# Twelve-layer decoder on one core: the additive mask of two cross-attentions moves from TensorE into VectorE's maximum

## The chip, the cores and the metric

The kernel runs on one core of a Trainium2 chip. The metric is the device time of one execution in microseconds (us). Engines are named as in the profile: PE is TensorE's matmul, PEld its weight load, DVE is VectorE, ACT is ScalarE, POOL is GpSimd, SP is SyncE, which issues the transfers here.

## What is computed

A decoder of four blocks, each with a self-mixing layer, a cross-attention to a context of 154 rows and a feed-forward layer; each of the twelve is followed by a residual and a layer norm. There are 4 batch elements, 512 rows, width 128, and 16 heads of width 8. The change touches the four cross-attentions. The masked ones (L1 and L3) are, cut to what matters:

```python
def _L1_xattn_ref(q, k, v, mask, Wq, bq, Wk, bk, Wv, bv, Wo, bo):
    qh, kh, vh = (proj(q, Wq, bq), proj(k, Wk, bk), proj(v, Wv, bv))
    scores = jnp.einsum('bhqd,bhkd->bhqk', qh, kh) / jnp.sqrt(jnp.float32(D_K))
    scores = jnp.where(mask[:, None] == 0, jnp.float32(-1000000000.0), scores)
    attn = jax.nn.softmax(scores, axis=-1)
    ctx = jnp.einsum('bhqk,bhkd->bhqd', attn, vh)
    concat = ctx.transpose(0, 2, 1, 3).reshape(bs, -1, INPUT_DIM)
    return concat @ Wo.T + bo

x = _layernorm(x + _L1_xattn_ref(x, ctx_1024, ctx_1024, mask_BxSxS2_ik1, ...), axis=-1)
```

L3 is the same without biases and with a mask of the other sense. L2 has biases and no mask. L0 has neither mask nor output projection, and an inner layer norm with gamma and beta: `x = z + decoded`, normed, times gamma plus beta, before the outer residual and norm.

## The kernel before

**Layers and pieces.** Every layer is a generator that yields small pieces. The driver runs the pieces of one layer in its main phase, and between two layers it mixes the tail of the old one with the start of the new one by a hand-written pattern of letters. Engines take their instructions in the order in which the pieces record them; nothing is reordered later, so each engine has a fixed queue.

**A cross-attention (`cross_attention`, L816)** works on 16 units per layer: a batch element times a group of four heads. Two things are computed for the scores of a unit. First (`half`, with a = n + 2) the scores with rows on the partitions, `scx`, from which only the row maxima are taken. Later (with n) the transposed scores `stx`, from which ScalarE takes the exponentials `pTx`. Between them the negated maxima `top` are split into three bf16 parts on GpSimd (`split_maxima`, L488 to L491), turned over on TensorE (`link_maxima`, L499) and added on VectorE into spare rows of the query operand (L501), so that the matmul of the transposed scores subtracts the maximum by itself.

**A step n** (`step`) records in this order: half 0 (scores of unit n + 2, transposed scores of unit n), `sums` (L991, products with the values for unit n − 1), `link_maxima` for n + 1, agenda pieces (division of an older unit's output, output projection and norm once per batch element, preparation of the next one), half 1, `more_sums` (L1000), `left` (L977, L979, the last 26 keys), `split_maxima` for n + 2. Steps run from −2; units 0 and 1 get their maxima in steps −2 and −1.

**One half of a masked layer before the change.** For each of two pairs of row tiles (qp) a PSUM tile `scx` of 128 x (2 x 2 x 154) f32 is taken. `psum2` hands these out in turn from two buffers, so a half's tiles are those of the half before it. TensorE first writes the mask into each (L936, identity times the bf16 mask `mq`, 308 columns, 2 matmuls per tile), then the mask into `stx` (L945), then adds the scores (L950: 8 matmuls of 154 columns, 4 per tile) and the transposed scores (L958). VectorE then takes one maximum over each tile:

```python
for qp, sc in enumerate(scs):
    nc.vector.tensor_reduce(
        ops.maxima(a)[:, 2 * qp : 2 * qp + 2, 2 * gp : 2 * gp + 2].rearrange("p i r -> p r i"),
        sc, AX.X, ALU.max, negate=True,
    )
```

**Other places.** L0's output path (`more_sums`, shuffled form): VectorE transposes (L1012) and takes reciprocals (L1014), GpSimd divides (L1015); once per batch element GpSimd adds the residual (L1026), VectorE takes the statistics, and GpSimd applies the norm (L1030 through `applied`, L346), gamma, beta and the residual. `send` (L396) projects queries or keys into PSUM, ScalarE adds the bias and scales (L408), with a scaled copy of the bias from VectorE where the scale is not one (L406), and GpSimd splits the result in three (L409 to L412) for transfers that SP issues (L416). The sends for L2's cross-attention are recorded during the layer before it (L2_attn).

Of the kernel before, what the change touches and what calls it, by code (L numbers as in the profile page):

```python
# [12 lines left out]
BF16 = mybir.dt.bfloat16  # L13
# [3 lines left out]
ALU = mybir.AluOpType  # L17
# [4 lines left out]
P = 128  # L22
B, S, D = 4, 512, 128
NT = S // P
H, DK = 16, 8
KC = 154
# [148 lines left out]
def decoder_kernel(ctx: ExitStack, tc: tile.TileContext, x, ctxT, mask1, mask3, packs, offsets, out, layers):  # L175
# [217 lines left out]
    Q_ROWS, K_ROWS = ((1, 1, 3), (6, 1, 2), (0, 1, 1)), ((0, 3, 3), (1, 6, 2), (2, 1, 1))  # L393
    SLOT = 32

    def send(far, order, w, rhs, scale, bias, raw, part, on=nc.gpsimd, by=nc.sync):  # L396

        n = rhs.shape[-1]
        pj = psum_t("ps_proj", kind="a" if "a" in ring else "t")
        nc.tensor.matmul(pj[:, :n], lhsT=w, rhs=rhs, start=True, stop=True)  # L400
        if bias is None:
            nc.scalar.activation(raw, pj[:, :n], AF.Copy, scale=scale)
        else:
            if scale != 1.0:
                scaled_bias = small.tile([P, 1], F32, tag="sb", name="sb", bufs=2)
                nc.vector.tensor_scalar(scaled_bias, bias, scale, None, ALU.mult)  # L406
                bias = scaled_bias
            nc.scalar.activation(raw, pj[:, :n], AF.Identity, bias=bias, scale=scale)  # L408
        on.tensor_copy(part[:, 0, :], raw)  # L409
        on.tensor_tensor(raw, raw, part[:, 0, :], ALU.subtract)  # L410
        on.tensor_copy(part[:, 1, :], raw)
        on.tensor_tensor(part[:, 2, :], raw, part[:, 1, :], ALU.subtract)  # L412
        for i, (at, gap, m) in enumerate(order):
            for r in range(2):
                rows = far[r].rearrange("(s k) p c -> (k p) s c", k=DK)
                by.dma_start(  # L416
                    rows[:, at : at + gap * (m - 1) + 1 : gap, :],
                    part[64 * r : 64 * r + 64, i : i + 1, :].to_broadcast([64, m, n]),
                )
# [7 lines left out]
    def sends(i, x_T):  # L427

        name, w = layers[i], weights[layers[i]]
        if name.endswith("xattn"):  # L430
            scale = 1.0 if name == "L0_xattn" else DK ** -0.5

            def key(b):
                return lambda room: send(
                    far_kc[b], K_ROWS, w["wk"], ctx_sb[:, b, :], 1.0, w.get("bk"), *room(KC)
                )

            def query(b):
                return lambda room: send(
                    far_q[i % 2][b], Q_ROWS, w["wq"], x_T[:, b, :], scale, w.get("bq"), *room(S)  # L440
                )

            return [x for b in range(B) for x in ((-1, ("k", b), key(b)), (b, ("q", b), query(b)))]
        if name == "L3_attn":
            xd = []

            def down(room):
                xd.append(room("xd"))
                pd = psum_t("xd", kind="a" if "a" in ring else "t")
                nc.tensor.matmul(pd, lhsT=w["wd"], rhs=x_T[:, 0, :], start=True, stop=True)  # L450
                evacuate(xd[0], pd)

            scale = DK ** -0.25
            return [
                (0, "down", down),
                (0, ("q", 0), lambda room: send(far_q[i % 2][0], Q_ROWS, w["wq"], xd[0], scale, None, *room(S))),
                (0, ("k", 0), lambda room: send(far_k[0], K_ROWS, w["wk"], xd[0], scale, None, *room(S))),
            ]
        return []
# [356 lines left out]
    def cross_attention(w, cur, new, last, room, scale, mask=None, shuffled=False):  # L816
# [15 lines left out]
        made = {}  # L832
        agenda = Agenda()
        units = 4 * B

        def masks(b):
            bt = slice(b * NT, (b + 1) * NT)
# [88 lines left out]
        def half(a, n, gp):  # L926

            scs, sts = [], []
            if a is not None:
                ma, ja = made[a // 4], a % 4  # L930
                for qp in range(2):
                    sc = psum2("scx")[:, :, : 2 * KC].rearrange("p r (i k) -> p r i k", k=KC)
                    scs.append(sc)
                    if mask is not None:
                        for r in range(2):
                            nc.tensor.matmul(  # L936
                                sc[:, r], lhsT=identb, rhs=ma["mq"][:, 2 * qp : 2 * qp + 2, :], start=True,
                                stop=False, skip_group_check=True,
                            )
            if n is not None:  # L940
                mn, jn = made[n // 4], n % 4
                sts = [psum_a("stx") for r in range(2)]
                if mask is not None:
                    for st in sts:
                        nc.tensor.matmul(st, lhsT=identb, rhs=mn["mT"], start=True, stop=False, skip_group_check=True)  # L945
            for qt in range(NT):
                for r in range(2):
                    if a is not None:
                        rows = slice(64 * r, 64 * r + 64)
                        nc.tensor.matmul(  # L950
                            scs[qt // 2][:, r, qt % 2, :], lhsT=ma["q"][rows, 2 * ja + gp, qt * P : (qt + 1) * P],
                            rhs=ma["k"][rows, 2 * ja + gp, :], start=(mask is None), stop=True,
                            skip_group_check=True,
                        )
                for r in range(2):
                    if n is not None and qt == 0:
                        rows, p = slice(64 * r, 64 * r + 64), 2 * jn + 1 - gp
                        nc.tensor.matmul(  # L958
                            sts[r], lhsT=mn["k"][rows, p, :P], rhs=mn["q"][rows, p, :],
                            start=(mask is None), stop=True, skip_group_check=True,  # L960
                        )
            for qp, sc in enumerate(scs):
                nc.vector.tensor_reduce(  # L963
                    ops.maxima(a)[:, 2 * qp : 2 * qp + 2, 2 * gp : 2 * gp + 2].rearrange("p i r -> p r i"),
                    sc, AX.X, ALU.max, negate=True,
                )
            for r, st in enumerate(sts):
                pT = work[0].tile([P, S], F32, tag="pTx", name="pTx", bufs=8)
                nc.scalar.activation(pT, st, AF.Exp)  # L969
                weights_of[n, 2 * (1 - gp) + r] = pT  # L970
# [25 lines left out]
        def more_sums(n):  # L996
            b, j = divmod(n, 4)
            m = made[b]
            av = m["av"]
            nc.tensor.matmul(  # L1000
                av, lhsT=m["v2"][:, j].rearrange("p g k -> p (g k)"), rhs=weights_of.pop((n, 4)),
                start=False, stop=True, skip_group_check=True,
            )
            if not shuffled:
                avs = copied(av, keep)
                agenda.add(n + 2, [lambda: divided(avs, m["o"], j)])
                if j == 3:
                    agenda.add(n + 3, out_pieces(b, m["o"], w, keep, cur, new, last, split=True))
                return

            ot = keep.tile([P, 16, 32], F32, tag="ot", name="ot", bufs=2)
            nc.vector.transpose(ot.rearrange("p s k -> p (s k)"), av.rearrange("p (q s) -> p s q", s=16))  # L1012
            rec = small.tile([P, 16], F32, tag="recx", name="recx")
            nc.vector.reciprocal(rec, ot[:, :, DK])  # L1014
            nc.gpsimd.tensor_tensor(  # L1015
                m["zt"][:, j, :].rearrange("p (s d) -> p s d", d=DK), ot[:, :, :DK],
                rec[:, :, None].to_broadcast([P, 16, DK]), ALU.mult,
            )
            if j == 3:
                zt = m["zt"]  # L1020
                xs = cur["x"][:, b * NT : (b + 1) * NT, :]
                ys = keep.tile([P, NT, D], F32, tag="ys", name="ys")
                stats = []

                def inner():
                    nc.gpsimd.tensor_tensor(zt, zt, xs, ALU.add)  # L1026
                    stats.extend(ln_stats(zt, NT, "i"))

                def outer():
                    applied(ys, zt, NT, *stats, on=nc.gpsimd)  # L1030
                    nc.gpsimd.tensor_tensor(ys, ys, w["gamma"][:, None, :].to_broadcast([P, NT, D]), ALU.mult)
                    nc.gpsimd.tensor_tensor(ys, ys, w["beta"][:, None, :].to_broadcast([P, NT, D]), ALU.add)
                    nc.gpsimd.tensor_tensor(ys, ys, xs, ALU.add)

                agenda.add(n + 2, [inner, outer] + finish_pieces(b, ys, new, last, split=True))
# [1370 lines left out]
```

## Time and profile before

| what | value |
|---|---|
| median of 3 runs (lowest, highest) | 2720.16 us (2719.19, 2727.39) |
| time of the profiled execution | 2720.02 us |
| its span, first to last instruction | 2718.2 us |
| PE busy, share of the span | 2445.7 us, 90% |
| DVE busy | 1681.6 us, 62% |
| ACT busy | 1251.3 us, 46% |
| POOL busy | 1071.5 us, 39% |
| mean granted TensorE clock | 0.954 |
| first and last row of the mask matmuls L936 | start at 846.5 and 2429.5 us |
| rows of L0's division L1015 | start at 273.1 to 375.3 us |

The page gives busy times as shares of the whole span; the layers have different limits, so what a change in one layer is worth is read from windows cut inside that layer. The two masked cross-attentions lie at about 845 to 985 us (L1) and 2305 to 2450 us (L3); L0's lies at about 245 to 390 us. A group row gives the line, engine, operation, output and inputs with shapes, then count, busy time and mean duration, then idle time of the engine just before and what ended it.

### The profile page before, as it was taken

To read this page: it belongs to the slowest core of one execution; us is meant where nothing else is said; L and a number is where in the kernel's file an instruction comes from. 1 tells how busy PE (TensorE), PEld (TensorE's weight loads), DVE (VectorE), ACT (ScalarE), POOL (GpSimd) and SP (SyncE) were. 2 spreads that over 40 slices of the span, in tenths; PEclk is the share of its full clock that TensorE was granted. 3 is DMA by queue.
4 is the path that set the end of the run, shared out by engine and by line. 5 is a ranking of instruction groups with operands and counts; after the bars stand their busy time and mean duration, and the time that the engine had idled before them with its cause. 6 is when DMAs were issued, how large, how long until landed. Compare 5 with 4: busy or idle time off the path is not lost. (4 is left out here: it accounts for less than half of the span.)

```text
span 2718.2 us, 38015 instructions
## 1 busy us (share of the span) xinstructions
PE 2445.7 (90%) x14378; PEld 1179.3 (43%) x14378; DVE 1681.6 (62%) x2872; ACT 1251.3 (46%) x2533; POOL 1071.5 (39%) x1406
## 2 busy tenths in 40 slices
PE   5898789988877989999999999998988999899998
PEld 1233234433333444444444555554455233445665
DVE  6796741188997665555445555556755887664444
ACT  3775432377652433333233555553543777343221
POOL 2342540157675326555452444443355342320000
PEclk7998989989989999999999999998997899899999
DMA  5421310000002400000000000002102240410000
GB/s 153 116 79 57 100 35 0 1 0 1 0 16 75 146 7 1 1 1 1 1 1 1 15 10 3 12 13 72 49 1 59 71 120 20 132 33 1 5 5 8
DMA packets 75559, 96.40 MB, mean 35 GB/s; under 512 B 23664, under 2 KB 62320, under 8 KB 75376
## 3 DMA queue, kind: packets, MB, share of 16 engines
q1 hardware_dynamic: 74224, 92.14, 11.7%
q8 instruction: 113, 1.85, 0.3%
q10 hardware_dynamic: 1152, 1.84, 0.2%
q14 instruction: 70, 0.57, 0.1%
HBM read 63.92 MB, written 33.49 MB: 36 GB/s over the span
## 5 line engine op out<-in xcount | busy, mean ns | idle before, releaser
L1164 POOL TENSOR_TENSOR pr<-pr,zs 128x1024 f32<-128x1024 f32 x192 | 237.1, 1252 | 234.2 <-DVE zs L1161 185.4
L670 DVE TENSOR_REDUCE top<-sc 128x2 f32<-128x1024 f32 x256 | 300.8, 1215 | 46.1 <-PE sc L666 43.2
L691 ACT ACTIVATE pT<-st 128x512 f32<-128x512 f32 x512 | 276.2, 598 | 88.2 <-PE st L682 85.1
L1155 ACT ACTIVATE pr<-scc,nm 128x256 f32<-128x256 f32 (+3 forms) x384 | 198.2, 526 | 173.2 <-DVE nm L1149 107.7
L1149 DVE TENSOR_REDUCE nm<-scc 128x2 f32<-128x1024 f32 x192 | 153.5, 820 | 167.5 <-PE scc L1137 166.3
L963 DVE TENSOR_REDUCE top<-scx 128x4 f32<-128x616 f32 x256 | 191.4, 791 | 90.1 <-PE scx L950 79.2
L969 ACT ACTIVATE pTx<-stx 128x512 f32<-128x512 f32 x256 | 139.1, 596 | 213.4 <-PE scx L950 128.2
L2137 POOL TENSOR_TENSOR hh<-hh,cs 128x1024 f32<-128x1024 f32 x64 | 149.3, 2354 | 74.5 <-DVE hh L2133 50.2
L1288 DVE TENSOR_TENSOR vtmp<-psve,gm 128x1024 f32<-128x1024 f32 x64 | 78.3, 1224 | 153.7 <-PE psve L1283 58.4
L705 PE MATMUL av<-pT,vbuf 128*32 128x256 f32 x2048 | 162.8, 393 | 8.6 <-ACT avs L505 8.6
L337 POOL TENSOR_TENSOR rsf<-mvf,eps 128x4 f32<-128x4 f32 x48 | 9.8, 204 | 394.3 <-DVE mvf L335 393.3
L488 POOL CAST nmP<-top 128x16 bf16<-128x16 f32 x96 | 25.3, 264 | 344.4 <-DVE top L963 180.3
L1131 PE MATMUL scc<-k,q 64*128 64x512 f32 (+3 forms) x768 | 143.9, 472 | 6.5 <-ACT pr L1155 2.7
L1180 PE MATMUL ptc<-ident,pr 128*128 128x128 f32 x960 | 137.8, 281 | 10.5 <-POOL pr L1164 8.9
L2133 DVE TENSOR_TENSOR_SCAN hh<-da,pb 128x1024 f32<-128x1024 f32 x64 | 142.6, 2269 | 0.0
L1293 POOL TENSOR_TENSOR vtmp<-vtmp 128x512 f32<-128x512 f32 x60 | 76.1, 1269 | 162.3 <-DVE vtmp L1288 137.7
L666 PE MATMUL sc<-kP,qP 64*128 64x512 bf16 x512 | 106.0, 412 | 33.9 <-DVE top L670 16.6
L1283 PE MATMUL psve<-w_L_ffn,xT 128*128 128x512 f32 x256 | 123.1, 605 | 14.5 <-ACT pr L1155 11.2
L2146 PE MATMUL acc<-hh,ident 128*128 128x512 f32 x256 | 132.9, 646 | 3.1 <-DVE yt L2155 1.9
L1193 PE MATMUL avc<-pT,v 128*64 128x512 f32 (+3 forms) x768 | 131.4, 449 | 0.5 <-DVE pT L1516 0.5
L1180 PEld LDWEIGHTS ptc<-ident,pr 128*128 128x128 f32 x960 | 103.1, 141 | 50.5 <-issue 26.4
L1326 PE MATMUL yT<-gT,w_L_ffn 128*128 128x512 f32 x256 | 123.4, 605 | 0.0
(417 smaller groups left out, 5065.1 us busy)
## 6 DMA issues: line engine op xcount, KB each, us to landing
qP<-far_q SPq DMA_DIRECT2D x24, 768.0 KB, 5.8
w_L_ffn<-in_L_ffn SPq DMA_DIRECT2D x24, 512.0 KB, 6.2
far_q<-part SPq DMA_DIRECT2D x44, 192.0 KB, 2.8
qP<-far_q SPq DMA_DIRECT2D x24, 256.0 KB, 4.2
far_q<-part SPq DMA_DIRECT2D x44, 128.0 KB, 2.4
kP<-far_k SPq DMA_DIRECT2D x7, 768.0 KB, 5.1
kP<-far_kc SPq DMA_DIRECT2D x16, 231.0 KB, 4.6
w_L_attn<-in_L_attn SPq DMA_DIRECT2D x6, 512.0 KB, 6.5
```

The costliest lines, as they stand in the source:

```text
L670: return lambda: nc.vector.tensor_reduce(top[:, qt, 2 * gp : 2 * gp + 2], sc, AX.X, ALU.max, negate=True)
L691: nc.scalar.activation(pT, st, AF.Exp)
L705: nc.tensor.matmul(m["av"][32 * g : 32 * g + 32, part], lhsT=m["v"][:, kt, 4 * j + g, :], rhs=weights_of[s, g][:, part], start=(kt == 0 an ...
L963: nc.vector.tensor_reduce(ops.maxima(a)[:, 2 * qp : 2 * qp + 2, 2 * gp : 2 * gp + 2].rearrange("p i r -> p r i"), sc, AX.X, ALU.max, negat ...
L969: nc.scalar.activation(pT, st, AF.Exp)
L1131: nc.tensor.matmul(sc[:, r, at : at + n], lhsT=q[rows, qt * P : n], rhs=k[rows, :n], start=(i == 0), stop=False, skip_group_check=True,)
L1149: nc.vector.tensor_reduce(nm[:, i, :], sc[:, :, at : at + (qt + 1) * P], AX.X, ALU.max, negate=True)
L1155: nc.scalar.activation(pr[:, r, at:to], sc[:, r, at:to], AF.Exp, bias=nm[:, i, r : r + 1], accum_out=zs[:, i, r : r + 1],)
L1164: nc.gpsimd.tensor_tensor(pr[:, :, at : at + n], pr[:, :, at : at + n], zs[:, i, :, None].to_broadcast([P, 2, n]), ALU.mult)
L1180: nc.tensor.transpose(pt[:, r, to : to + P], self.pr[u, p][:, r, lo : lo + P], ident)
L2133: nc.vector.tensor_tensor_scan(flat, das[g % 2][:, c].rearrange("p n t -> p (n t)"), pbs[c].rearrange("p n t -> p (n t)"), 0.0, ALU.mult, ...
L2137: nc.gpsimd.tensor_tensor(m["h", j][c], m["h", j][c], m["C", j], ALU.mult)
```

## The change

In the masked layers the mask is no longer written into `scx` by TensorE. The score matmuls start the accumulation themselves. In place of one `tensor_reduce` over a tile of four blocks of score rows there are four `tensor_tensor_reduce`, each of which adds 154 mask values to 154 scores, multiplies by −1, writes the elements to a tile that nobody reads (`unused`, one buffer) and takes the minimum into one column of `top`. The mask for the transposed scores (L945, L977) stays on TensorE. In L0 the division and the inner norm go from GpSimd to VectorE. In L2 the sends' bias and scale go from ScalarE to VectorE.

```diff
-    def send(far, order, w, rhs, scale, bias, raw, part, on=nc.gpsimd, by=nc.sync):
+    def send(far, order, w, rhs, scale, bias, raw, part, on=nc.gpsimd, by=nc.sync, biased=nc.scalar):
...
+        elif biased == nc.vector:
+            nc.vector.tensor_scalar(raw, pj[:, :n], bias, scale, ALU.add, ALU.mult)
         else:
             if scale != 1.0:
...
+            biased = nc.vector if name == "L2_xattn" else nc.scalar
...
+        unused = pool.tile([P, KC], BF16, name="unused", bufs=1) if mask is not None else None
...
-                    if mask is not None:
-                        for r in range(2):
-                            nc.tensor.matmul(
-                                sc[:, r], lhsT=identb, rhs=ma["mq"][:, 2 * qp : 2 * qp + 2, :], start=True,
-                                stop=False, skip_group_check=True,
-                            )
...
-                            rhs=ma["k"][rows, 2 * ja + gp, :], start=(mask is None), stop=True,
+                            rhs=ma["k"][rows, 2 * ja + gp, :], start=True, stop=True,
...
             for qp, sc in enumerate(scs):
+                if mask is not None:
+
+                    for i in range(2):
+                        for r in range(2):
+                            nc.vector.tensor_tensor_reduce(
+                                unused, sc[:, r, i], ma["mq"][:, 2 * qp + i, :], -1.0, 3.0e38, ALU.add, ALU.min,
+                                ops.maxima(a)[:, 2 * qp + i, 2 * gp + r : 2 * gp + r + 1],
+                            )
+                    continue
...
-            nc.gpsimd.tensor_tensor(
+            nc.vector.tensor_tensor(
                 m["zt"][:, j, :].rearrange("p (s d) -> p s d", d=DK), ot[:, :, :DK],
...
-                    applied(ys, zt, NT, *stats, on=nc.gpsimd)
+                    applied(ys, zt, NT, *stats)
```

In the built program each `tensor_tensor_reduce` is two VectorE instructions: one over 128 x 154, and one that writes a 128 x 1 column of `top`. Each of the first kind waits for a VectorE semaphore, because it writes the same `unused` as the one before.

| engine | instructions that go | instructions that come |
|---|---|---|
| PE | 256 matmuls L936, with their weight loads | none |
| DVE | 128 `tensor_reduce` over 128 x 616, 4 scaled biases | 512 over 128 x 154, 512 of 128 x 1, 16 divisions, 16 norm applications, 8 biases |
| ACT | 8 biases | none |
| POOL | 16 divisions, 16 norm applications | none |

More of the change, by code (lines that the diff above doesn't have):

```diff
@@ L431, in sends @@
             scale = 1.0 if name == "L0_xattn" else DK ** -0.5
+            biased = nc.vector if name == "L2_xattn" else nc.scalar
             def key(b):
                 return lambda room: send(
-                    far_kc[b], K_ROWS, w["wk"], ctx_sb[:, b, :], 1.0, w.get("bk"), *room(KC)
+                    far_kc[b], K_ROWS, w["wk"], ctx_sb[:, b, :], 1.0, w.get("bk"), *room(KC), biased=biased
                 )
@@ L439, in query @@
                 return lambda room: send(
-                    far_q[i % 2][b], Q_ROWS, w["wq"], x_T[:, b, :], scale, w.get("bq"), *room(S)
+                    far_q[i % 2][b], Q_ROWS, w["wq"], x_T[:, b, :], scale, w.get("bq"), *room(S), biased=biased
                 )
```

## The prediction

> **What bounds the kernel now.** I read the page's engine shares, then cut windows inside the two masked layers, and there read the chain of waits. The chain in L3's cross-attention (start us, us, what):
>
> ```profile
> 2349.80 0.63 PE scx L936 x4
> 2350.43 0.43 PE stx L945 x2
> 2350.86 0.17 PE scx L950 x2
> 2351.03 0.21 PE stx L958 x2
> 2351.25 0.20 PE scx L950 x6
> 2351.45 0.99 PE avx L991 x8
> 2352.44 0.55 PE pmx L499 x8
> 2353.00 0.44 PE pto L512 x4
> 2353.44 0.53 PE scx L936 x4
> ...
> 2356.59 0.63 PE scx L936 x4
> ```
>
> The chain never leaves PE: from one half 0 to the next, 2349.80 to 2356.59, is 6.79 us, and the mask matmuls L936 take 0.63 + 0.53 = 1.16 us of it. Here PE is the bound. The windows agree (length, PE, PEld, DVE, ACT, POOL busy, granted clock, DMA share, GB/s):
>
> ```profile
> 2360.00:2380.00 20.00, 20.00 (x166) 9.96 (x165) 12.17 (x25) 10.26 (x19) 7.81 (x17) 1.00 0.38 112
> 2380.00:2400.00 20.00, 19.72 (x177) 10.06 (x175) 14.42 (x33) 8.03 (x16) 5.75 (x16) 1.00 0.29 93
> ```
>
> PE is full, DVE has 6 to 8 us free in each 20. What is taken away is therefore on the path; the question is whether what is added fits DVE's free time. The groups that this rests on:
>
> ```profile
> L963 DVE TENSOR_REDUCE top<-scx 128x4 f32<-128x616 f32 x256 | 191.4, 791 | 90.1 <-PE scx L950 79.2 <-POOL part L412 5.9 <-POOL ml L852 3.6
> L936 PE MATMUL scx<-mq,identb 128*128 128x308 bf16 x256 | 47.3, 302 | 7.8 <-DVE top L963 7.2 <-DVE mq L839 0.4
> L516 DVE TENSOR_TENSOR o<-pto,rec 128x128 f32<-128x128 f32 x80 | 23.3, 291 | 2.8
> L1952 DVE SCALAR_TENSOR_TENSOR ys<-ype,o,ys 128x128 f32<-128x128 f32 x112 | 31.5, 344 | 35.3 <-PE ype L1940 35.3
> L406 DVE TENSOR_SCALAR sb<-w_L_xattn 128x1 f32<-128x1 f32 x8 | 1.1, 134 | 0.0
> ```
>
> **A step of DVE before.** I count L963's rows by windows. L3, 2340 to 2420 us: 42 reductions; four make a step, so 10.5 steps, 7.62 us each. DVE was busy 51.3 us there, 30.95 of them in L963; the rest is 20.4 / 10.5 = 1.94 us per step (adding the maxima, divisions, norms, value copies). L1, 860 to 960 us: 51 reductions, 12.75 steps, 7.84 us each; DVE 61.8, L963 38.3, the rest 1.84 per step. Means: a step of 7.73 us, 1.89 us of other DVE work, 2.97 us of reductions. The plain steps of the chain are shorter (6.79) than the mean because preparation and output work comes once in four.
>
> **Mask matmuls removed.** 1.16 us of PE per step: PE's floor becomes 7.73 − 1.16 = 6.57 us.
>
> **The new reduction: 16 pairs per step in place of 4 reductions.** The trace has no such operation. Let c be the time from the start of one pair to the next; DVE then needs 1.89 + 16c per step. Equal to today's 7.73 at c = 0.365; equal to PE's new floor at c = 0.29. What rows give for c: a main part over 154 elements. L516 is two tensors, one in PSUM, 128 elements: 291 ns; 26 more at the slope of L963 against the 1024-wide reduction of L670 (1215 − 791 ns over 408 elements, 1.04 ns each) make 318. L1952, the nearest three-operand form, gives 344 + 27 = 371. I take 345. The 128 x 1 part: L406, 134 ns; a two-column reciprocal (L1161) has 156. I take 140. How neighbours space out is seen in a row of statistics, where the second waits for the first and the third waits for nothing:
>
> ```profile
> 2465.41 0.26 DVE L334 BATCH_NORM_STATS2 st<-ys 128x6 f32<-128x128 f32 x1
> 2465.71 0.18 DVE L335 BATCH_NORM_AGGREGATE mvf<-st 128x2 f32<-128x6 f32 x1
> 2465.80 0.26 DVE L334 BATCH_NORM_STATS2 st<-ys 128x6 f32<-128x128 f32 x1
> ```
>
> With a wait it starts 0.04 us after the end (2465.67 to 2465.71); without one, 0.09 us before the end (2465.89 against 2465.80). A pair has one of each: the read does not wait by a semaphore, the next main part does. So c = 0.345 − 0.08 + 0.14 + 0.035 = **0.44 us**. From below: 0.318 − 0.08 + 0.06 (a read half as long as the shortest row) + 0.035 = 0.335. From above: 0.371 + 0.156 with a wait on both sides, 0.60.
>
> [...] The rows give 0.44. [...]
>
> **Does DVE really run through?** A `scx` tile comes free only when its four pairs are done. With 8c = 3.5 us per half, PE writes the first tile of the next half while DVE works on the second of this one, then stands at the second until DVE frees it. After that it needs about 0.3 us for scores, 0.99 for L991, 0.55 for the turned maxima and 0.44 for the next division: 2.3 us, inside the 3.5 us that DVE spends on this half's pairs. GpSimd's split of the maxima takes about 1.25 us (four operations of 230 to 270 ns), also inside. So DVE always finds work, and PE stands behind it; queued behind PE's stalled score matmuls are `stx`, `sums` and `pmx`, none late by DVE's count. The step is DVE's sum: 1.89 + 16 x 0.44 = 8.93 us, which is 1.20 more than 7.73. Of 16 steps per layer with reductions, 14 lie in the main phase: 28 x 1.20 = **+34 us**.
>
> **Steps −2 and −1** of both layers, four in all: DVE gets 16 x 0.44 − 2.97 = 4.1 us more in each, PE 1.16 less. They lie among another layer's tail and waits for transfers, with DVE at 12.6 of 20 us (840 to 860) and 6.8 of 20 (2300 to 2320). Bounds: 4 x −1.2 and 4 x 4.1, so −5 and +16; I take +1.5 each, **+6 us**, since DVE's idle time there hides most.
>
> **L0: division and norm to DVE.** POOL loses 16 x 406 + 16 x 793 ns = 19 us, DVE gains 16 x 0.29 (L516's size) + 16 x 0.28 (four applications take 1.11 us elsewhere) = 9 us. From 250 to 390 us DVE was busy 95 of 140 us and PE 106, so neither is full; DVE's free time hides it. Against: the transposes L1012 queue behind the division, and PE waited for them 13.1 us in all. For: the split of maxima no longer queues behind 3.1 us of norm on POOL, and the hand-over from DVE to POOL goes. Bounds −6 and +9, taken **0**.
>
> **L2's biases.** Eight on DVE at the nearest row, L1469 (tensor by scalar from PSUM, 512 wide, 750 ns): 4 x 0.75 + 4 x 0.38, less 4 x 0.13 for scaled biases: +4 us; ACT −4 us (688 and 390 ns each). From 1850 to 1912 us DVE was busy 40.6 of 62, so it is hidden: **0**, at most +4 if DVE were full there. POOL's splits and SP's transfers keep their order, one hand-over later or earlier by under 0.1 us.
>
> **Sum.** +34 + 6 = +40 us on the profiled execution's 2720.02 us (span 2718.2), which agrees with the median 2720.16: **2760 us**.
>
> **Rivals.** Forecast, DVE takes over as bound with c of 0.38 to 0.51: 0.66. (1) Same bound, larger price: the read has to wait until the main part has drained and each of the two costs a full instruction, c = 0.53 to 0.60: 28 x (1.89 + 8.5 − 7.73) + 10 gives +84 at 0.53, 2804 us, and 2835 at 0.60. For it: every pair is serial through one tile. Against: no wait stands before the read. 0.12. [...] 0.11. (3) The other side, in the masked main phase: a pair costs no more than 0.29 us because main part and read overlap with their neighbours, PE stays the bound and its 1.16 us is kept: 28 x −1.16 = −32, 2688 us. It decides from c below 0.345, where the loss in the first steps is paid for and 8 us remain. For it: DVE's 6 to 8 free us in 20. Against: one main part alone has 318 ns by the rows, and each waits for the last. 0.11, with what lies between it and (2). That the mask isn't taken off PE is excluded: the built program has 256 matmuls fewer.
>
> About 0.3%, 8 us, is what a measurement here tells from no change. Slower: 0.66 + 0.12 and a little of (2), 0.79. Within: 0.10. Faster: 0.11. [...]
>
> **What would show it.** In the profile after: pairs every 0.44 us; DVE at 19 of 20 us in the masked main phase, PE near 15; in the chain there, DVE's reductions in place of PE; PE's idle before L950 ended by DVE; a step near 8.9 us; L0 and L2 unmoved within 5 us. Wrong if PE is still full in those windows, or if the pairs are under 0.36 us.

## The result, and the profile after

| what | before | after |
|---|---|---|
| median of 6 runs (lowest, highest) | 2719.68 us (2718.69, 2727.39) | 2733.78 us (2729.84, 2738.55) |
| time of the profiled execution | 2720.02 us | 2736.12 us |
| its span | 2718.2 us | 2734.3 us |
| PE busy in the span | 2445.7 us | 2419.5 us |
| DVE busy in the span | 1681.6 us | 1764.8 us |

The ratio is 1.0046, 95% interval 1.0029 to 1.0062: slower, by some 13 us, a third of the 40 that were forecast. The whole says little here, because three effects of both signs lie in it. They part when the same row is looked up in both traces and its start compared (us from the span's start):

| mark | before | after | shift so far | stage in between |
|---|---|---|---|---|
| L0's last transpose | 374.2 | 362.3 | −11.9 | L0 cross-attention |
| first mask conversion of L1's cross-attention | 844.4 | 833.4 | −11.0 | L0's and L1's other layers |
| first value matmul of L1_ffn | 989.3 | 996.5 | +7.2 | **L1 cross-attention, masked: +18.2** |
| first query-key matmul of L2_attn | 1446.3 | 1452.8 | +6.5 | L1_ffn |
| last query-key matmul of L2_attn | 1836.3 | 1835.8 | −0.5 | **L2_attn, with L2's sends in it: −7.0** |
| last norm application on POOL, before L3's cross-attention | 2296.6 | 2295.1 | −1.5 | L2 and L3's self-mixing layer |
| first gate matmul of L3_ffn | 2448.7 | 2464.8 | +16.1 | **L3 cross-attention, masked: +17.6** |
| last gate matmul | 2701.4 | 2717.5 | +16.1 | L3_ffn |

The two masked layers lose 36 us. L0 and L2_attn give back 18 to 19, where the forecast had 0.

**The masked layers after.** The chain of waits in L3, of the changed kernel (start us, us, what; "issue" is time in which the engine waited for nothing that the profile shows):

```profile
2366.09 0.32 DVE unused L966
...
2366.48 0.21 issue
...
2366.77 0.61 DVE qP L505
...
2367.42 0.38 PE stx L944
2367.80 0.17 PE scx L949 x2
2367.97 0.22 PE stx L957 x2
...
2368.30 0.32 DVE unused L966
```

Before, this chain was PE alone. Now it runs through the rows of the new reduction, then through the query addition (L505), and then over to PE for the transposed scores and the next scores, and back. Between 2360 and 2372 us DVE's rows L966 are 67% of it. The same windows as in the prediction, after (length, PE, PEld, DVE, ACT, POOL, granted clock, DMA share, GB/s):

```profile
2360.00:2380.00 20.00, 16.94 (x136) 6.92 (x138) 15.90 (x89) 9.46 (x18) 4.46 (x14) 1.00 0.30 106
2380.00:2400.00 20.00, 17.14 (x147) 8.11 (x146) 16.71 (x92) 8.66 (x16) 6.10 (x14) 1.00 0.49 149
```

PE fell from full to 17 of 20 us, DVE rose by 2 to 4. Neither is full: what fills the rest of DVE's time is in its timeline. A pair is a main part (`CUSTOM_DVE_ANT_0`) and the read of its minimum (`DVE_READ_ACCUMULATOR2_ANT`); in brackets stands the idle time before a row and what ended it. One tile's four pairs and the first pair of the next:

```profile
2360.55 0.32 DVE L966 CUSTOM_DVE_ANT_0 unused<-scx,mq 128x154 bf16<-128x154 f32 x1 [0.43 <-PE scx L949]
2360.79 0.08 DVE L966 DVE_READ_ACCUMULATOR2_ANT top<- 128x1 f32 x1
2360.91 0.32 DVE L966 CUSTOM_DVE_ANT_0 unused<-scx,mq 128x154 bf16<-128x154 f32 x1
...
2361.63 0.32 DVE L966 CUSTOM_DVE_ANT_0 unused<-scx,mq 128x154 bf16<-128x154 f32 x1
2361.87 0.08 DVE L966 DVE_READ_ACCUMULATOR2_ANT top<- 128x1 f32 x1
2362.10 0.32 DVE L966 CUSTOM_DVE_ANT_0 unused<-scx,mq 128x154 bf16<-128x154 f32 x1
```

The read starts 0.08 us before the main part's end (2360.87 against 2360.79), takes 0.08, and the next main part starts 0.04 after it: 0.36 us from pair to pair. Where the tile changes it is 0.47 (2361.63 to 2362.10). The eight pairs of a half so take 7 x 0.36 + 0.47 = 2.99 us, 0.37 each. The group rows, and what PE waits for (L945 is the row of the kernel before that corresponds to L944):

```profile
L966 DVE CUSTOM_DVE_ANT_0 unused<-scx,mq 128x154 bf16<-128x154 f32 x512 | 163.1, 319 | 49.4 <-PE scx L949 23.6 <-DVE top L966 1.9
...
L949 PE MATMUL scx<-kP,qP 64*128 64x154 bf16 x1024 | 93.8, 248 | 49.1 <-DVE top L966 22.4 <-DVE top L971 14.2 <-issue 8.5
...
L944 PE MATMUL stx<-mT,identb 128*128 128x512 bf16 x126 | 43.7, 398 | 21.3 <-DVE qP L505 18.8 <-DVE ys L546 1.1 <-DVE xT L327 0.7
...
L945 PE MATMUL stx<-mT,identb 128*128 128x512 bf16 x128 | 40.0, 390 | 0.7 <-DVE xT L327 0.4 <-DVE ys L542 0.2
...
L966 DVE DVE_READ_ACCUMULATOR2_ANT top<- 128x1 f32 x512 | 42.4, 83 | 0.2
```

Two waits of PE stand out. L949 waits 22.4 us for the pairs to free a score tile, which was forecast (before, L936 waited 7.2 for the reductions). L944, the mask of the transposed scores, waits 18.8 us for the query addition, which was not forecast and is new: the PSUM tile of the turned maxima is one of three buffers that the program hands out in turn, and the second transposed-score tile of half 1 is the next to get it. The query addition frees it, and stands in DVE's queue behind the eight pairs of half 0. While PE stands there, the next scores stand behind it, and DVE runs dry: the 0.43 us in front of the first row above. In the 15 steps per layer of the next table DVE waited for scores 8.5 us in L1 and 7.8 in L3.

A step can be measured as the distance between two query additions, of which there is one per step. The last 15 distances of each masked layer, and of three experiments below:

| kernel | L1, 15 steps (us) | L3, 15 steps (us) | mean step | a plain step |
|---|---|---|---|---|
| before | 117.7 | 114.2 | 7.73 | 6.8 |
| after | 132.1 | 129.7 | 8.73 | 7.6 to 7.8 |
| e12, scores ahead | 127.8 | 125.9 | 8.46 | 7.1 to 7.2 |
| e6, half of the mask | 117.6 | 115.4 | 7.77 | 6.7 |
| e5, eight scratch tiles | 111.4 | 107.6 | 7.30 | 6.35 |

A lower granted clock is not what made most of the steps longer. In the last twelve of the 15 it was 0.98 (L1) and 1.00 (L3) after the change, 1.00 before, and these twelve grew by 10.4 and 10.9 us. In the first three it was 0.73 after, 0.93 and 0.86 before, and they grew by 4.0 and 4.6. What part of that is the clock's was not separated; e4 below, without the mask's edit, took 25.1 us for L1's first three at 0.77, the kernel before 24.8 at 0.93.

### The profile page after: what moved, and what is told of

Same layout as the page of the kernel before. It is cut to its first block, busy times and chain, and to the rows that moved or that the text cites. A ratio compares the mean times of both kernels' runs of the same rounds, so it can differ in the third digit from the quotient of the medians.

```text
span 2734.3 us, 38476 instructions
## 1 busy us (share of the span) xinstructions
PE 2419.5 (88%) x14102; PEld 1158.6 (42%) x14122; DVE 1764.8 (65%) x3804; ACT 1249.0 (46%) x2525; POOL 1055.9 (39%) x1374
## 5 line engine op out<-in xcount | busy, mean ns | idle before, releaser
L977 ACT ACTIVATE pTx<-stx 128x512 f32<-128x512 f32 x256 | 139.1, 596 | 214.6 <-PE scx L949 130.1
L966 DVE CUSTOM_DVE_ANT_0 unused<-scx,mq 128x154 bf16<-128x154 f32 x512 | 163.1, 319 | 49.4 <-PE scx L949 23.6
L670 PE MATMUL sc<-kP,qP 64*128 64x512 bf16 x512 | 106.6, 415 | 35.5 <-DMA qP<-far_q 16.1
L949 PE MATMUL scx<-kP,qP 64*128 64x154 bf16 x1024 | 93.8, 248 | 49.1 <-DVE top L966 22.4
```

Source lines behind the costliest of these rows:

```text
L966: nc.vector.tensor_tensor_reduce(unused, sc[:, r, i], ma["mq"][:, 2 * qp + i, :], -1.0, 3.0e38, ALU.add, ALU.min, ops.maxima(a)[:, 2 * qp ...
```

## The experiments

Ratios are to the kernel before, run beside each. The first four take the change apart.

**e1, the mask's edit alone.** L0 and L2 as before:

```diff
-            nc.vector.tensor_tensor(
+            nc.gpsimd.tensor_tensor(
                 m["zt"][:, j, :].rearrange("p (s d) -> p s d", d=DK), ot[:, :, :DK],
...
-                    applied(ys, zt, NT, *stats)
+                    applied(ys, zt, NT, *stats, on=nc.gpsimd)
...
-            biased = nc.vector if name == "L2_xattn" else nc.scalar
+            biased = nc.scalar
```

> Only the masked cross-attentions are changed; L0's division and norm stay on GpSimd and L2's biases on ScalarE. If the gain of L0 (11 us earlier at its end in the trace) and of L2_attn (7 us) comes from the other two edits, this kernel takes back both: 2720 + 18 + 18, about 2755 us, ratio 1.013, and L0 ends where it did before. If those shifts belong to something else, such as a disturbed clock or the mask's edit itself, it stays near 2734.

Measured 2753.22 us, ratio 1.0133 (1.0112 to 1.0154), which is +36 us on 2717.5. The mask's edit costs what the two masked stages show.

**e2, L0's two operations alone; e3, L2's biases alone; e4, both without the mask's edit.** These are the diff's own lines on the kernel before.

> Only L0's division and inner norm go to VectorE. Theory: GpSimd's queue was the limit of L0 at batch borders, because 3.1 us of norm stood ahead of the split of the maxima; then 2709 us, ratio 0.996, with L0 11 us shorter. Rival of the prediction, that neither engine was full and the move is hidden: 2720.

> Only L2's biases go to VectorE. Theory: in L2_attn the send's activation stood between the exponentials in ScalarE's queue, its result came late, and GpSimd's splits then stood ahead of the division that TensorE waits for; freed, 7 us: 2713, ratio 0.997. Rival of the prediction, hidden: 2720.

> L0's and L2's edits without the mask's. If the three parts add up: 2720 - 11 - 7 = 2702 us, ratio 0.9934, faster than both kernels. If the gains overlap, between 2702 and 2713.

Measured: e2 2707.91 us, ratio 0.9969 (0.9956 to 0.9982), −8 us. e3 2711.16, 0.9975 (0.9964 to 0.9986), −7 us. e4 2698.16, 0.9932 (0.9913 to 0.9952), −18 us. So both small edits are gains and add up within the intervals. With e1 they make the measured whole within the intervals: +36 − 18 = +18, where e1 has +30 to +42 and e4 −24 to −13, against +13 with +8 to +17.

**e5, no wait between pairs.** The unread elements go to eight tiles in turn:

```diff
-        unused = pool.tile([P, KC], BF16, name="unused", bufs=1) if mask is not None else None
+        unused = [pool.tile([P, KC], BF16, name=f"unused{i}", bufs=1) for i in range(8)] if mask is not None else None
...
-                                unused, sc[:, r, i], ma["mq"][:, 2 * qp + i, :], -1.0, 3.0e38, ALU.add, ALU.min,
+                                unused[4 * qp + 2 * i + r], sc[:, r, i], ma["mq"][:, 2 * qp + i, :], -1.0, 3.0e38, ALU.add, ALU.min,
```

> The changed kernel, but the elements that nobody reads go to eight tiles in turn, so that a pair needs no wait for the pair before it. Theory: VectorE's throughput is the bound of the masked layers. A pair then takes less than its 0.36 us; if 0.28, a step needs 1.9 + 16 x 0.28 = 6.4 us of VectorE, less than TensorE's 6.6, and the masked layers fall below their old time: 2734 - 36 - up to 32, so 2670 to 2700 us. Rival 1, the accumulator read holds the engine whatever is waited for: 0.36 stays, 2734. Rival 2, the layers are held by the transposed scores' wait for the query addition and not by VectorE's sum: gain under 10 us, 2725 to 2734.

Measured 2686.15 us, ratio 0.9879 (0.9865 to 0.9894): 45 us (by the ratios) to 48 us (by the medians) below the changed kernel, faster than before and than e4. In its timeline the pairs stand closer:

```profile
2350.00 0.31 DVE L966 CUSTOM_DVE_ANT_0 unused<-scx,mq 128x154 bf16<-128x154 f32 x1
2350.24 0.08 DVE L966 DVE_READ_ACCUMULATOR2_ANT top<- 128x1 f32 x1
2350.24 0.32 DVE L966 CUSTOM_DVE_ANT_0 unused<-scx,mq 128x154 bf16<-128x154 f32 x1
```

Both parts last as long as before (0.31 to 0.32 and 0.08), but the read and the next main part start together, and the pair costs 0.24 us instead of 0.36. What the wait on one scratch tile cost was 512 x 0.12 = 61 us of DVE, and without it the kernel is 45 to 48 us faster. (The run takes away the shared tile and the wait for it together, so the two were not told apart.) Both rivals fall: the read doesn't hold the engine, and DVE's pairs, not the query addition alone, were what held the step. The step doesn't reach PE's floor, though: 6.35 us in plain steps against 6.79 − 1.16 = 5.63, and in the mean 0.43 us of the 1.16 arrive (7.73 to 7.30). Neither engine is full in its 30 steps: PE was busy 196.9 and DVE 176.5 of 219.0 us. What holds the step there was not found; e9 and e13 below tried the query addition and gained nothing.

**e6, the mask of the first tile on VectorE, of the second on TensorE**, in the changed kernel with one scratch tile:

```diff
+                    if mask is not None and qp == 1:
+                        for r in range(2):
+                            nc.tensor.matmul(
+                                sc[:, r], lhsT=identb, rhs=ma["mq"][:, 2 * qp : 2 * qp + 2, :], start=True,
+                                stop=False, skip_group_check=True,
+                            )
...
-                if mask is not None:
+                if mask is not None and qp == 0:
```

> The changed kernel, but only the first of the two score tiles of a half gets its mask on VectorE; the second is masked by TensorE and reduced by one instruction as before. Theory, each engine's sum decides: VectorE 1.9 + 1.5 + 8 x 0.39 = 6.5 us per step, TensorE 7.73 - 0.58 = 7.15: TensorE bound, 28 x -0.58 = -16 us against a kernel with L0's and L2's edits alone, 2682 us. Rival, any mask on VectorE costs because pairs come in bursts that hold the score tiles: between 2698 and 2734, about 2716 in proportion.

Measured 2703.56 us, ratio 0.9939 (0.9922 to 0.9956), not to be told from e4 (0.9913 to 0.9952), and 12 below the rival's proportion. The theory of plain sums fails: a plain step took 6.73 us, where PE's sum has 6.79 − 0.58 = 6.2 and DVE's, in the mean step, 1.89 + 1.49 + 8 x 0.36 = 6.3. PE's transposed scores wait for the query addition here too, but six times and 1.8 us in all from 2340 to 2420, which is too little to explain it. The cause stays open.

**e7, L0's division alone; e8, L0's norm alone** (one run each):

> Only L0's division goes to VectorE, the norm stays on GpSimd. Theory, the norm in GpSimd's queue is what held L0: a gain of 2 us or less, L0's last transpose within 3 us of 374. Rival, the hand-over at each unit: 16 x 0.4 = 6 us or more.

> Only L0's inner norm goes to VectorE. Theory, the norm in GpSimd's queue is what held L0: three batch borders give back 2 to 3 us each, L0's last transpose 8 us or more before 374. Rival, the hand-over of the division: under 5 us.

Measured: e7 2707.72 us with the last transpose at 363.0; e8 2714.70 us with it at 369.5; before 2718.87 us and 374.2. My theory had the two the wrong way round: the division is the larger part (11 us in the trace against 5).

**e11, the division stays on GpSimd, but behind the split of the maxima.** This asks why the division matters.

```diff
-            nc.gpsimd.tensor_tensor(
+            waiting.append(lambda: nc.gpsimd.tensor_tensor(
                 m["zt"][:, j, :].rearrange("p (s d) -> p s d", d=DK), ot[:, :, :DK],
                 rec[:, :, None].to_broadcast([P, 16, DK]), ALU.mult,
-            )
+            ))
...
                 ops.split_maxima(a)
+            while waiting:
+                waiting.pop(0)()
```

> The kernel before, with the division of L0 still on GpSimd but recorded behind the split of the maxima instead of ahead of it. Theory: the division did no harm by its 0.41 us, but by standing at the head of GpSimd's queue until VectorE's reciprocal comes, with the split behind it: 2706 to 2711 us, as with the division on VectorE. Rival: the operation's own time and hand-over: 2716 to 2720.

Measured 2712.97 us, ratio 0.9970 (0.9962 to 0.9978): as much as e2 within the intervals, with no work taken off GpSimd. L0's last transpose starts at 367.0, 7.2 us earlier than before; e2's starts at 364.5, 9.7 earlier. In the table of waits of the kernel before, from 262 to 385 us (engine line waited for: us in total, times, longest):

```profile
PEld L499 <- POOL nmP L491: 29.5, 13, 7.3
POOL zt L1015 <- DVE recx L1014: 28.0, 12, 4.8
...
PE pmx L499 <- POOL nmP L491: 17.0, 12, 6.4
```

GpSimd stood 28 us with the division at the head of its queue and VectorE's reciprocal not yet there, and the split of the maxima, which needs neither, stood behind it. One unit of the kernel before:

```profile
283.25 0.79 DVE L963 TENSOR_REDUCE top<-scx 128x4 f32<-128x616 f32 x1
...
285.03 0.41 POOL L1015 TENSOR_TENSOR zt<-ot,recx 128x128 f32<-128x128 f32 x1 [3.81 <-DVE recx L1014]
285.38 0.26 POOL L488 CAST nmP<-top 128x16 bf16<-128x16 f32 x1
```

The maxima are there at 284.04, the split starts at 285.38. So not all of the 28 us is lost, since GpSimd would have waited for the maxima anyway: in this unit 1.3 us are. PE waited 17.0 us for the split. In e11, over the same stretch:

```profile
PEld L499 <- POOL nmP L491: 12.0, 4, 7.0
...
PE pmx L499 <- POOL nmP L491: 8.5, 2, 6.1
```

**e9 and e10, the query addition between the two tiles' pairs**, with eight scratch tiles and with one. The second tile's pairs of half 0 become a function that the step calls after `link_maxima`:

```diff
-            half(a, now, 0)
+            rest = half(a, now, 0)
...
                 ops.link_maxima(n + 1)
+            for f in rest:
+                f()
```

> The kernel with eight scratch tiles (2686 us), but in half 0 the query addition is recorded between the four pairs of the first score tile and those of the second, not behind all eight. Theory: what holds its step at 6.35 us with both engines below that is the second transposed-score tile of half 1, which takes the PSUM buffer that the query addition has to free. Then the addition ends 0.3 to 0.6 us earlier and the step shrinks by as much: 28 x 0.3 = 8 us, 2672 to 2682. Rival: VectorE then stands idle for the turned maxima, and nothing is gained: 2684 to 2692.

> The changed kernel (one scratch tile) with the query addition between the first and the second tile's pairs. Theory: VectorE's own sum is the bound there, and moving the wait gains at most the 0.43 us gap per step: 2722 to 2734. Rival: the wait for the query addition, not VectorE's sum, makes the masked layers slower: most of the 36 us comes back, about 2705.

Measured: e9 2703.95 us, ratio 0.9931 (0.9908 to 0.9954), 18 us worse than e5. e10 2741.45, 1.0071 (1.0050 to 1.0093), worse than the changed kernel. Both times lie outside what theory and rival had; e9's rival named the right wait, but took it for small. The edit trades one wait for another. In the 30 steps of the two layers DVE waits 24.2 us for the turned maxima (L505 for PE's L503) in e9, where it waited 6.2 in e5, which is as much more as the whole loss. In e10 it is 21.7 us, in the changed kernel 5.1. Plain steps stayed at 6.32 us in e9 against 6.35.

**e12 and e13, scores ahead of the transposed scores** in TensorE's queue, with one scratch tile and with eight. This leaves DVE's sum as it is and takes away only its dry time.

```diff
-                sts = [psum_a("stx") for r in range(2)]
-                if mask is not None:
-                    for st in sts:
-                        nc.tensor.matmul(st, lhsT=identb, rhs=mn["mT"], start=True, stop=False, skip_group_check=True)
+                if mask is None:
+                    sts = [psum_a("stx") for r in range(2)]
...
+            if n is not None and mask is not None:
+                sts = [psum_a("stx") for r in range(2)]
+                for st in sts:
+                    nc.tensor.matmul(st, lhsT=identb, rhs=mn["mT"], start=True, stop=False, skip_group_check=True)
...
```

> The changed kernel (one scratch tile), but in the masked layers TensorE's queue has the scores of a half ahead of its transposed scores. Theory: a part of the 36 us is not VectorE's sum but the time in which VectorE stands dry, because the next scores are queued behind a transposed-score tile that waits for the query addition; then the 0.4 to 0.6 us per step come back, 28 x 0.5 = 14 us: 2716 to 2724. Rival: VectorE's sum alone is the bound, 2730 to 2736.

> The same order with eight scratch tiles, against 2686 us without it. Theory: with pairs of 0.24 us the wait for the query addition holds the step at 6.35 us in plain steps; with the scores ahead of it TensorE's floor of 5.6 to 6.0 comes into reach: 28 x 0.4 = 11 us, 2670 to 2680. Rival: ScalarE's exponentials come later and hold the values' matmuls instead, 2682 to 2690.

Measured: e12 2725.98 us, ratio 1.0019 (1.0009 to 1.0029), 7 to 8 us better than the changed kernel where 14 were expected. Its timeline has the dry time gone in a plain step:

```profile
2361.91 0.29 DVE L520 TENSOR_TENSOR o<-pto,rec 128x128 f32<-128x128 f32 x1
2362.07 0.39 PE L965 MATMUL stx<-qP,kP 64*128 64x512 bf16 x2
2362.12 0.31 DVE L974 CUSTOM_DVE_ANT_0 unused<-scx,mq 128x154 bf16<-128x154 f32 x1
```

The division ends at 2362.20 and the next pair has already started. Plain steps fell by 0.5 us, as expected; some of the other steps became longer (9.4 and 9.7 us in L1, where the changed kernel has 8.1 and 8.7), which ate half of it. Over the 30 steps DVE's waits for scores fell from 16.3 to 3.9 us, but its waits for the turned maxima rose from 5.1 to 9.8: TensorE now stands at the scores until DVE frees a score tile (34.8 us over the run, 22.4 in the changed kernel), and the turned maxima stand behind them. e13 took 2688.67 us, 0.9884 (0.9867 to 0.9900), no better than e5: plain steps of 6.07 us against 6.35, and longer ones elsewhere. There the waits for scores fell from 16.7 us in e5 to at most 4.4, those for the turned maxima rose from 6.2 to 22.5.

## Why the prediction was right and wrong

The forecast was 34 + 6 + 0 + 0 = 40 us. The two terms taken as 0 are what failed in the sum: L0 and L2 gave back 18 to 19. The first two came out at 36, and that was in part luck. The range put on record, 2712 to 2808 us, holds the measured 2733.78; one ground of its lower end, a low price of the pair, is shown by no run: the trace has 0.36 to 0.37 us.

**Right: where the path goes, and the loss of the masked layers.** PE was the bound there, DVE's pairs took its place in the chain, and the loss was named as 34 + 6 us. The 15 step distances of the two layers grew by 14.4 and 15.5 us, 30 in all, and the rest of the two stages by 3.8 and 2.1, 6 in all (the distances begin in step −1, so the two cuts are not quite the same). e1 has +36.

**Wrong inside that term: two sizes that cancel, by luck.** DVE was to be at 19 of 20 us and PE near 15; they are at 15.9 to 16.7 and at 17. The step is 8.73 us, as forecast (8.9), but made up otherwise. The pair was put at 0.44 us and is 0.36, 0.37 with the tile changes. The main part was guessed at 345 ns: the two-tensor row, carried to 154 elements, gave 318, and 319 was measured; the step up to the three-operand row was not called for. The read was put at 140 ns from the shortest row and is 83. With 5.98 us for 16 pairs DVE's sum is 1.89 + 5.98 = 7.87 us per step, where 8.93 was forecast: 0.14 above the old step, and only some 4 of the 30 us. Most of the other 0.86 us per step was in a place that the prediction declared free: "So DVE always finds work" did not look at which PSUM buffer the transposed scores get. The wait of L944 for L505 holds up the next scores, and DVE waits for these 16.3 us in the 30 steps, 0.54 per step. e12 shows that this wait can be removed, and that a plain step then gains 0.5 us. The remaining 0.3 us per step are in shorter waits that were not followed up.

**Wrong: L0, the term "division and norm to DVE", taken as 0 with bounds −6 and +9.** It is −12 in the trace of the changed kernel and −8 in e2. The sum compared busy times and called both engines free. What GpSimd's division did was to stand at the head of a queue until VectorE's reciprocal came, 28 us in all, and that wait stood in the table of waits before the change. I named the queue behind the norm (3.1 us, four times) and missed the queue behind the division, which stands there 16 times. The 13.1 us set against the gain are nearly one wait counted twice: PE's for the transposes (6.0) plus that of its weight loads (7.1), at the same moments.

**Wrong: L2's biases, taken as 0, at most +4.** They are −7. The window from 1850 to 1912 us, in which the prediction found DVE free, holds only the last of the eight sends; the other seven start between 1497 and 1825, in L2_attn. There the send's activation stood in ScalarE's queue behind the exponentials and a 1.02 us copy, and its result came late. In L2_attn of the kernel before:

```profile
1725.34 0.72 ACT L408 ACTIVATE raw<-ps_proj,sb 128x512 f32<-128x512 f32 x1
...
1729.84 3.03 POOL L1164 TENSOR_TENSOR pr<-pr,zs 128x768 f32<-128x768 f32 x3
...
1731.93 0.66 PE L1180 MATMUL ptc<-ident,pr 128*128 128x128 f32 x4 [1.86 <-POOL pr L1164]
```

and after, at the same place of the program (3.3 us later in the trace):

```profile
1727.47 0.75 DVE L404 TENSOR_SCALAR raw<-ps_proj,w_L_xattn 128x512 f32<-128x512 f32 x1 [1.59 <-PE ps_proj L400]
...
1732.01 3.03 POOL L1172 TENSOR_TENSOR pr<-pr,zs 128x768 f32<-128x768 f32 x3
...
1734.10 0.66 PE L1188 MATMUL ptc<-ident,pr 128*128 128x128 f32 x4 [0.73 <-POOL pr L1172]
```

On VectorE the operation (0.75 us) starts right behind the projection, 1.2 us earlier when counted from the projection's start. GpSimd's four splits of the sent rows so end 1.1 us earlier, the softmax's division that GpSimd has queued behind them starts as much earlier, and TensorE's turn of its result idles 0.73 us instead of 1.86. Over all of L2_attn this idle time of TensorE (L1180 waiting for L1164) falls from 8.0 to 3.2 us, in the changed kernel and in e3 alike, which is 4.8 of the 7 us. That the edit gains 7 us is shown by e3; that the place in ScalarE's queue is the reason is read from the traces, and no run moved that alone. The prediction wrote "POOL's splits [...] keep their order, one hand-over later or earlier by under 0.1 us": it counted the hand-over and not the place in ScalarE's queue.

**The rivals.** A larger price (0.53 and more) and a pair of 0.29 us with one scratch tile are both excluded by 0.36. The second rival, with 0.11, took a cheap pair, DVE and PE about level, and no change in the time. No run shows the price that it set out from; the runs showed 0.36 to 0.37 us, by which DVE's sum, 7.87 us per step, is about level with the old step of 7.73. The time did not stay, though: the masked layers still lose 36 us, through waits that no sum of busy times holds. The mechanism of the third rival, read and main part overlapping with their neighbours, is what e5 shows at 0.24 us once the wait is gone.

## What to carry to other kernels

When an operation moves between engines, ask first where it stood in the queue that it leaves. L0's division, 0.41 us long, waited for another engine and held up the split behind it by 1.3 us in the unit shown; its busy time says nothing of that, the table of waits does. A scratch output that nobody reads can still be a dependency: here one shared scratch tile, with the waits for it, cost a third of each pair (0.36 against 0.24 us with eight). And DVE's free time did not make the work there free: the pairs stood ahead of the query addition, which frees a PSUM buffer that TensorE needs (18.8 us of waits).

The version that beats both kernels is e5: 2686.15 us, ratio 0.9879 (0.9865 to 0.9894). It is the whole change, with eight scratch tiles in place of one.

## What was not expected of the hardware

A wait for an instruction of the same engine, with the one tile that both write, cost 0.12 us per pair on VectorE, a third of the pair, though the instruction waited for was the one just ahead in the same queue: without it, in e5, the next main part starts together with the read (2350.24 both), with it 0.12 after the read's start (2360.79, 2360.91). And the new operation with two inputs, one in PSUM in f32 and one in bf16, and an output and a running minimum, takes 319 ns for 154 elements, no longer than the plain two-tensor row of the trace carried to that width (318).
